# Layer 0 of a four-layer convolution stack: 128 KB transfers in one queue, spread over each slot's products

## The chip, the cores and the metric

The kernel runs on one core of a Trainium2 chip. Its five engines run their own instruction streams: TensorE (PE; its weight loads are shown apart as PEld), VectorE (DVE), ScalarE (ACT), GpSimd (POOL) and SyncE (SP). Transfers between DRAM and the on-chip memory (SBUF) are issued by SP and by ACT and run on 16 DMA engines. The metric is the device time of one execution in microseconds (us). Lower is better.

## The reference, cut to what matters

The input x has 4 images of 16 frames of 512 x 512 float32. Four layers follow, each "x + f(groupnorm(x))". Only layer 0 is touched by the change. It treats the frames as a time series: each output frame is made from a frame and its two neighbours.

```
def _conv_reflect(x, w, bias, dil, pad):
    xp = jnp.pad(x, ((0,0),(0,0),(pad,pad),(pad,pad)), mode='reflect')
    out = conv(xp, w, rhs_dilation=(dil, dil))        # 3 channels in, 1 out, 5 x 5 taps
    return out + bias

def _denoise_block(x, w1, b1, w2, b2, w3, b3, a, b, c):
    trip = _triplets(x)                               # frames t-1, t, t+1
    o = a * _conv_reflect(trip, w1, b1, 1, 2) + b * _conv_reflect(trip, w2, b2, 2, 4) + c * _conv_reflect(trip, w3, b3, 4, 8)
    return jnp.tanh(o)

# layer 0
y = _denoise_block(_gn(x), ...blk1...)
z = _denoise_block(y, ...blk2...)
x = x + z
# layers 1 to 3: x + conv3x3(quantised gn(x)), x + box17x17(gn(x)), x + fft-convolution(gn(x))
```

## The kernel before

Layer 0 goes image by image. For each image the first convolution (`conv` 0, x to y) is done in four groups of four frames, and then the second (`conv` 1, y to z) in four groups: 32 groups in all. A group has six **slots**, p = 0 to 5, so there are 192 slots. In each slot TensorE forms one product (`products`, line 499): 14 steps n of 16 matmuls in 32 x 32 tiles, which the chip runs as 448 matmul instructions. The six products of a group are combined on DVE (a fast algorithm for the three taps in time), so DVE makes six combined frames before (`early`, `late`, `zeroth`, lines 446 to 484) and puts the results together after (`gather`, lines 510 to 552). ACT applies tanh (`activated`). The order of all instructions is written out by hand: each engine runs its stream in exactly the order in which `slot` (line 633) emits it.

PSUM has two product buffers, so product s+2 needs the product of slot s to be gathered. Frames sit in ten SBUF buffers. Tiles of x come from a pool `x` of six buffers of 512 KB (`xr` frames to convolve, `rim` borders, `xs` for the statistics of the next image, `xb` for the final addition). Results y and the reordered z share a pool `rb` of two buffers.

What moves, and on which queue:

- **Loads on SP, through `load` (line 198).** A half of an x frame is one transfer of 512 KB (`load_half`, line 212). A frame of y (`y_frame`, line 390) comes back from DRAM as eight transfers of 132 KB, six edge columns of 16.5 KB and two small ones for the mirrored border. Two shuffles on DVE (lines 409 and 410) then mirror the border columns; they are emitted right behind these loads, in the same slot.
- **Spacing.** `products` keeps the last matmul of each of its 14 steps as a mark. `load` counts the bytes of the slot and makes each transfer wait for one of these marks, one mark further per 190,000 bytes (`PACE`):

```
at = self.marks[min(self.moved // PACE, len(self.marks) - 1)]
self.tc.add_manual_dep(ins, at.name, AFTER, reason="transfers spread over the slot")
```

- **Stores on ACT.** A frame of y leaves in the slot after it is made, in two halves of the partitions, 528 KB each (`y_out`, line 578), at two places of ACT's stream. A frame of the result x1 (`z_out`, line 588) passes three slots: its `xb` halves are loaded where z is transposed, in the next slot `finish` adds on DVE, and one slot later `leave` issues two stores of 512 KB from ACT and sums for the statistics. In an image's last group `leave` comes with `finish`. None of these stores waits for a mark.

`later(n, f, what)` puts a function into slot now + n, where `do(what)` runs it at one of four places of the slot ("stores", "rows", "rest", "last"). `fetch` (line 417) requests frames for the next group: in the second convolution's middle groups frame 2 in p = 0, frame 4 in p = 1, frame 3 in p = 2, frame 5 in p = 4. Results come out in the order i = 2 (p = 4), 1 (p = 5), 0 (p = 0 of the next group), 3 (p = 1).

Of the kernel before, what the change touches and what calls it, by code (L numbers as in the profile page):

```python
# [20 lines left out]
P = 128  # L21
B, C, H, W = 4, 16, 512, 512
# [11 lines left out]
ORDER = (1, 2, 3, 4, 0, 5)  # L34
KN = 9 * 264
NFRAMES = 10
PACE = 190000
AFTER = mybir.DependencyInfo(mybir.DependencyClass.Sync, mybir.DependencyReason.SCHED_ONLY)
HELD = 6

# [81 lines left out]
class Layer0:  # L122
# [12 lines left out]
    def __init__(self, k, ctx, x1):  # L135
        self.k, self.tc, self.nc, self.a, self.x1 = k, k.tc, k.nc, k.a, x1
        tc = self.tc
        self.pools = {}
        for name, bufs in (("frames", 1), ("w", 1), ("sum", 1), ("ra", 2), ("rb", 2), ("x", 6), ("ek", 1)):
            self.pools[name] = ctx.enter_context(tc.tile_pool(name=f"l0{name}", bufs=bufs))  # L140
        self.psum = ctx.enter_context(tc.tile_pool(name="l0ps", bufs=2, space=PSUM))
        self.mv = k.stats.tile([P, NBG, 2], F32, name="mv1")
        self.top = k.stats.tile([P, B, C, 2], F32, name="top1")
        self.low = k.stats.tile([P, B, C, 2], F32, name="low1")
        self.frame_is = k.load(k.stats, "c_frame_is")
        self.parity = k.load(k.stats, "c_parity")
# [4 lines left out]
        self.marks, self.moved = [], 0  # L151


    def weights(self):
# [40 lines left out]
            self.nc.scalar.dma_start(self.w[q][PX * i : PX * i + PX], self.w_dram[conv, :, q])  # L195


    def load(self, to, src):

        ins = self.nc.sync.dma_start(to, src).ins  # L200
        if self.marks:
            at = self.marks[min(self.moved // PACE, len(self.marks) - 1)]
            self.tc.add_manual_dep(ins, at.name, AFTER, reason="transfers spread over the slot")
        self.moved += 4 * int(np.prod(src.shape))

    def load_x(self, b, t, half, name):

# [2 lines left out]
        return xt  # L210

    def load_half(self, xt, b, t, half):
        self.load(xt, self.a["x"][b, t].rearrange("(p T s) w -> T p (s w)", T=2, s=2)[half])

    def finish_stats(self, b, mv, lo=0):

# [62 lines left out]
    def rest_of_first(self, n, p):  # L279

        if n == -1 and p == 0:
            for t in (HELD, HELD + 1):
                self.load_ahead(t)
        for _ in range(1 if n < 0 and p < 4 else 2):
# [46 lines left out]
    def load_rims(self, b, t0):  # L331

        nc = self.nc
        raw = self.pools["x"].tile([P, 2, W], F32, name=f"rim_{b}_{t0}", tag="x")
        x = self.a["x"][b, t0 : t0 + 4]
        for r in range(4):
            for side in range(2):
                at = PX * r + 16 * side
                if (r, side) in ((0, 0), (3, 1)):
                    for s in range(2):  # L340
                        top = 8 - s if side == 0 else H - 2 - s
                        rows = x[:, top : top - 7 if top > 7 else None : -2, :]
                        self.load(raw[at : at + 16, s, :], rows)
                else:
                    r0 = P * r - 8 if side == 0 else P * r + P
                    self.load(
                        raw[at : at + 16].rearrange("p s w -> p (s w)"),
                        x[:, r0 : r0 + 8, :].rearrange("f (m s) w -> f m (s w)", s=2),
                    )
        return raw  # L350
# [39 lines left out]
    def y_frame(self, t):  # L390

        nc = self.nc
        fr = self.free.pop(0)
        v, y = fr.rearrange("p (k r) -> p k r", r=264), self.y[t]
        for c in range(4):
            at = PX * c
            lo, hi = slice(at, at + 16), slice(at + 16, at + PX)
            self.load(v[lo, 1:9], y[hi])
            self.load(v[hi, 0:8], y[lo])
            if c > 0:  # L400
                self.load(v[lo, 0], y[at - 16 : at, 7])
            if c < 3:
                self.load(v[hi, 8], y[at + PX : at + PX + 16, 0])

        self.load(v[0:9:8, 0], y[16:25:8, 0])
        self.load(v[119:P:8, 8], y[103:112:8, 7])
        left = [16 + p + 8 - 2 * (p % 8) if p < 16 and p % 8 else p for p in range(PX)]
        right = [p - 16 + 6 - 2 * (p % 8) if p >= 16 and p % 8 < 7 else p for p in range(PX)]
        nc.vector.stream_shuffle(v[0:PX, 0], v[0:PX, 0], left)
        nc.vector.stream_shuffle(v[96:P, 8], v[96:P, 8], right)  # L410
        return fr


# [72 lines left out]
    def products(self, gr, p):  # L486
# [4 lines left out]
        self.marks, self.moved = [], 0  # L491
# [86 lines left out]
    def y_out(self, gr, i):  # L578
# [1 line left out]
        for to, odd in gr["rim"]:  # L580
            self.stt(to, odd, self.parity[:, 1:2], to)
        gr["rim"].clear()
        y, z = self.y[4 * gr["g"] + i], gr["out"].pop((i, 0))
        for n, what in enumerate(("stores", "rows")):
            at = slice(64 * n, 64 * n + 64)
            self.later(1, partial(nc.scalar.dma_start, y[at], z[at]), what)

    def z_out(self, gr, i):

        nc, b, t = self.nc, gr["b"], 4 * gr["g"] + i  # L590
        zr = self.pools["rb"].tile([P, 2, 2, W], F32, name=f"zr_{b}_{t}", tag="rb")
        xs = []
        for h in range(2):
            z = gr["out"].pop((i, h))
            nc.vector.transpose(zr[:, h].rearrange("p s (k j) -> p k s j", j=16), z.rearrange("p (k r) -> p k r", r=32))
            xs.append(self.load_x(b, t, h, "xb"))

        def finish():
            for h in range(2):
# [10 lines left out]
        def leave():  # L610
# [21 lines left out]

    def slot(self, n, p):

        self.now = 6 * n + p
# [45 lines left out]
    def begin(self, gr):  # L681
# [1 line left out]
        if gr["conv"]:  # L683
            self.out_sums = [self.k.stats.tile([P, 2 * C], F32, name=f"osum{b}_{i}", tag=f"osum{i}") for i in range(2)]
        else:
            self.y = scratch(self.k.dram, f"y_{b}", [C, P, 8, 264])

    def run(self):
        self.groups = [
            {"b": b, "conv": conv, "g": g, "d": {}, "v": {}, "m": {}, "out": {}, "rim": []}  # L690
            for b in range(B)
            for conv in range(2)
            for g in range(4)
# [5 lines left out]
        with self.tc.manual_schedule():  # L699
            self.first()  # L700
            for g in range(-1, n + 1):
                for p in range(6):
                    self.slot(g, p)
                    if g < 1:
                        self.rest_of_first(g, p)
        return self.result()

    def result(self):
# [919 lines left out]
```

## Time and profile before

| what | value |
|---|---|
| median of 3 runs | 5569.73 us (5559.56 to 5571.75) |
| the profiled execution, its own time | 5572.08 us |
| its span | 5570.3 us |
| mean granted TensorE clock | 0.978 |
| first matmul of layer 0 | 80.7 us |
| last matmul of layer 0 | 3177.3 us |
| bytes moved | 860.92 MB, 155 GB/s on average |

One execution is taken apart. PE, PEld, DVE, ACT and POOL have busy times; a row of the groups gives line, engine and operation, the tile written and the tiles read, the number of instructions, busy us and mean ns, and behind the second bar the idle time just before them with what ended it. "Issue" there means idle time in which the engine waited for nothing that the profile shows. q1 is SP's transfer queue, q10 is ACT's, and q8 carries instructions. SPq and ACTq are the issuing of transfers. A row of waits gives the waiting engine and line, what it waited for, total us, number, and the longest.

Two lines of the chain of work that ended last say which engine and which lines carry the end:

```profile
PE 84%; issue 5%; ACT 4%; DVE 4%; DMA 2%; SPq 1%; ACTq 0%; DVEq 0%
PE m L499 50%; PE l1p L915 10%; PE l2p L999 5%; PE u L1464 4%; PE s L1405 4%; PE u L1405 4%; PE u L1427 2%; PE pt L1439 2%; ACT l2n L1017 2%; ACT l2s L1056 2%; PE l2p L1051 1%; SPq L200 1%; DVE frame L415 1%; DMA frame<-y 0%; PE pr L1449 0%
```

### The profile page before, as it was taken

Reading aid. Unit: us, or ns where it says so; the run is one execution under the profiler, and the core shown is the slowest. Engines: PE = TensorE matmul, PEld = TensorE weight load, DVE = VectorE, ACT = ScalarE, POOL = GpSimd, SP = SyncE. Lnnn points to the kernel's source line nnn. Section 1 sums busy time; section 2 is a strip of 40 time slices with the busy share of each in tenths; the row PEclk is TensorE's granted clock in tenths of the full one; section 3 lists DMA queues with packets and bytes.
Section 4 is the critical chain, followed back from the end, with each engine's and each line's share of the span. In section 5 each row is a group of like instructions: output and inputs, shape, how many; then the busy total and the mean of one; then the engine's idle time right before and its main releaser. Section 6 shows DMA issues by size and latency. Waiting matters only on the chain.

```text
span 5570.3 us, 267073 instructions
## 1 busy us (share of the span) xinstructions
PE 5105.7 (92%) x125040; PEld 3556.9 (64%) x125040; DVE 4044.1 (73%) x4738; ACT 2611.6 (47%) x4143; POOL 6.1 (0%) x18
## 2 busy tenths in 40 slices
PE   3999999999999989989999788887999979999999
PEld 2665665666675656666666545554887866777776
DVE  7766889657987659897678854445555568888887
ACT  2533335433345523443122444443665656666665
POOL 0000000000000000000000000000000000000000
PEclk9999999999999999999999999998999999999999
DMA  5555545565445555544454377876565655555554
GB/s 192 136 147 129 153 139 153 142 150 137 122 151 160 142 131 143 150 124 118 89 132 126 117 198 209 214 209 191 199 214 192 214 176 137 143 145 149 148 144 119
DMA packets 373827, 860.92 MB, mean 155 GB/s; under 512 B 52209, under 2 KB 74353, under 8 KB 356081
## 3 DMA queue, kind: packets, MB, share of 16 engines
q1 hardware_dynamic: 317072, 694.76, 44.1%
q10 hardware_dynamic: 55648, 149.08, 9.4%
q8 instruction: 979, 16.04, 1.3%
q14 instruction: 128, 1.04, 0.1%
HBM read 503.74 MB, written 339.90 MB: 151 GB/s over the span
## 4 chain that ended last, share of the span: by engine, by line
PE 84%; issue 5%; ACT 4%; DVE 4%; DMA 2%; SPq 1%; ACTq 0%; DVEq 0%
PE m L499 50%; PE l1p L915 10%; PE l2p L999 5%; PE u L1464 4%; PE s L1405 4%; PE u L1405 4%; PE u L1427 2%; PE pt L1439 2%; ACT l2n L1017 2%; ACT l2s L1056 2%; PE l2p L1051 1%; SPq L200 1%; DVE frame L415 1%; DMA frame<-y 0%; PE pr L1449 0%
## 5 line engine op out<-in xcount | busy, mean ns | idle before, releaser
L499 PE MATMUL m<-frame,l0w 32*32 32x512 f32 x86016 | 2920.8, 608 | 257.1 <-issue 151.7
L499 PEld LDWEIGHTS m<-frame,l0w 32*32 32x32 f32 x86016 | 1968.4, 104 | 1208.6 <-issue 604.0
L415 DVE SCALAR_TENSOR_TENSOR frame<-frame,frame 128x2376 f32<-128x2376 f32 x232 | 606.6, 2625 | 4.7 <-PE m L499 0.4
L915 PE MATMUL l1p<-l1q,l_wt 32*32 32x512 f32 x12288 | 489.2, 603 | 109.6 <-issue 68.1
L915 PEld LDWEIGHTS l1p<-l1q,l_wt 32*32 32x32 f32 x12288 | 274.4, 103 | 266.0 <-issue 186.0
L1039 DVE TENSOR_TENSOR l2o<-l2x,l2p 128x512 f32<-128x512 f32 x256 | 172.6, 674 | 283.1 <-PE l2p L999 283.1
L617 ACT ACTIVATE junk<-xb,neg 128x1024 f32<-128x1024 f32 x256 | 294.1, 1149 | 80.1 <-DVE top L601 38.2
L532 ACT COPY C<-m 128x1024 f32<-128x1024 f32 x64 | 61.6, 1014 | 537.2 <-PE m L499 408.7
L999 PE MATMUL l2p<-k_c_band,l2n 128*128 128x144 f32 (+1 forms) x2048 | 275.1, 295 | 36.5 <-DMA l2x<-x 15.5
L999 PEld LDWEIGHTS l2p<-k_c_band,l2y 128*128 128x128 f32 x2048 | 256.8, 190 | 75.0 <-issue 54.3
L999 PEld LDWEIGHTS l2p<-k_c_band,l2n 128*128 128x128 f32 x2048 | 262.2, 197 | 48.6 <-ACT l2n L1017 41.4
L999 PE MATMUL l2p<-k_c_band,l2y 128*128 128x144 f32 (+1 forms) x2048 | 284.3, 292 | 6.0
L901 DVE TENSOR_SCALAR l1t<-l1t 128x2048 f32<-128x2048 f32 x64 | 78.5, 1226 | 271.2 <-ACT l1t L900 271.2
L900 ACT ACTIVATE l1t<-l1x,l1own,l1own 128x1024 f32<-128x1024 f32 x128 | 151.8, 1233 | 237.4 <-DMA l1x<-x 234.6
L1464 PE MATMUL u<-k_c_hil,zt 128*128 128x128 f32 x2048 | 256.0, 279 | 0.0
L384 DVE STREAM_TRANSPOSE frame<-xp 128x1056 f32<-128x1056 f32 x128 | 161.6, 1278 | 127.0 <-ACT xp L358 127.0
L1464 PEld LDWEIGHTS u<-k_c_hil,zt 128*128 128x128 f32 x2048 | 238.5, 192 | 2.1 <-issue 0.8
L1440 ACT COPY zt<-pt 128x512 f32<-128x512 f32 x256 | 131.5, 601 | 210.3 <-PE pt L1439 210.3
L1028 ACT COPY l2y<-l2p 128x512 f32<-128x512 f32 x256 | 149.7, 585 | 169.1 <-PE l2p L999 169.1
L1370 DVE TENSOR_TENSOR xc<-l3n,k_c_tab 128x2048 f32<-128x2048 f32 x64 | 146.7, 2292 | 109.6 <-ACT l3n L1354 109.6
L915 PE MATMUL l1p<-l1x,l_wt 32*32 32x512 f32 x4088 | 213.3, 632 | 0.0
L1483 DVE SCALAR_TENSOR_TENSOR l3o<-u,l3t 128x256 f32<-128x256 f32 x512 | 192.8, 430 | 23.4 <-ACT l3t L1475 21.0
(302 smaller groups left out, 6553.0 us busy)
## 6 DMA issues: line engine op xcount, KB each, us to landing
y<-y ACTq DMA_DIRECT2D x128, 528.0 KB
frame<-y SPq DMA_DIRECT2D x512, 132.0 KB
xb<-in_x SPq DMA_DIRECT2D x128, 512.0 KB
x<-xb ACTq DMA_DIRECT2D x128, 512.0 KB
x<-l1o SPq DMA_DIRECT2D x256, 256.0 KB
l2x<-x SPq DMA_DIRECT2D x64, 1024.0 KB
x<-l2o SPq DMA_DIRECT2D x64, 1024.0 KB
l3x<-x SPq DMA_DIRECT2D x256, 256.0 KB
```

The source lines that it names most:

```text
L384: nc.vector.transpose(v[:, :, 4 + h : 68 : 2], xp)
L415: self.nc.vector.scalar_tensor_tensor(o, x, f, y, ALU.mult, ALU.add)
L499: ins = nc.tensor.matmul(ps[PX * j : PX * j + PX, i, :].rearrange("p (k r) -> p k r", r=64), w[rows, n], v[rows, k0 : k0 + 8, r0 : r0 + 64 ...
L617: nc.scalar.activation(junk, xs[h], f, bias=neg, accum_out=self.out_sums[n][:, 2 * t + h : 2 * t + h + 1])
L900: nc.scalar.activation(t[:, at], x[:, at], AF.Identity, bias=own[1], scale=own[0])
L915: nc.tensor.matmul(ps[32 * j : 32 * j + 32, b, :], wt[rows, a, d], qs[v % 3][rows, k, d : d + W] if d < 3 else raws[v][rows, k], start=(n ...
L999: nc.tensor.matmul(ps[:, lo:hi], lhs[:, k, at : at + P], band[:, j : j + hi - lo], start=(k == 0), stop=(k == 3), skip_group_check=True,)
L1028: nc.scalar.copy(yts[i][:, wb, :], ps)
L1039: nc.vector.tensor_add(o[:, hb, :], xt[:, hb, :], ps)
L1405: nc.tensor.matmul(ps[b][32 * j : 32 * j + 32], f[rows, n, j, :], x[rows, j, :], start=(i == 0), stop=(i == 2 and tag == "s"), skip_group_ ...
L1464: nc.tensor.matmul(po[:, bass.ts(k, P)], zt[:, b, k ^ 1, :], hil[:, k, :], start=False, stop=(k == 3), skip_group_check=True,)
L1483: nc.vector.scalar_tensor_tensor(o[:, v].rearrange("p k u -> p u k"), po[:, HW:W].rearrange("p (u k) -> p u k", u=2), s, t.rearrange("p (u ...
```

## The change

- All loads of layer 0 are collected per slot, and so are the y stores and most x1 stores. At the end of the slot `transfers` issues them from SP, loads first and then stores. Each waits for the mark that lies as far in the slot as its bytes lie in the slot's sum.
- A half of an x frame moves in four pieces of 32 partitions (128 KB), and so does a half of x1. A frame of y is stored in four pieces of 264 KB, each with two of the eight columns of all partitions.
- y in DRAM gets a pitch of 536 floats for every 528, and its loads are written as rows of 528 floats (2,112 bytes) in place of 2,112 floats (8,448 bytes).
- The two mirror shuffles run one slot after the loads.
- The xb loads come one slot earlier, except in an image's last group and for i = 3. The y store of i = 3 comes three slots after the frame is made, in place of one.
- While an image's last group is under way and in the group behind it (`last_of_image`), x1 stores stay on ACT in 512 KB.

```diff
-    def load(self, to, src):
-
-        ins = self.nc.sync.dma_start(to, src).ins
-        if self.marks:
-            at = self.marks[min(self.moved // PACE, len(self.marks) - 1)]
-            self.tc.add_manual_dep(ins, at.name, AFTER, reason="transfers spread over the slot")
-        self.moved += 4 * int(np.prod(src.shape))
+    def move(self, to, src, what="loads"):
+
+        if self.moves is None:
+            self.nc.sync.dma_start(to, src)
+        else:
+            self.moves[what].append((to, src))
+
+    def transfers(self):
+
+        moves = self.moves["loads"] + self.moves["stores"]
+        sizes = [int(np.prod(src.shape)) for _, src in moves]
+        for n, (to, src) in enumerate(moves):
+            ins = self.nc.sync.dma_start(to, src).ins
+            if self.marks:
+                at = self.marks[len(self.marks) * sum(sizes[:n]) // sum(sizes)]
+                self.tc.add_manual_dep(ins, at.name, AFTER, reason="transfers spread over the slot")
+        self.moves = {"loads": [], "stores": []}
...
     def load_half(self, xt, b, t, half):
-        self.load(xt, self.a["x"][b, t].rearrange("(p T s) w -> T p (s w)", T=2, s=2)[half])
+        src = self.a["x"][b, t].rearrange("(p T s) w -> T p (s w)", T=2, s=2)[half]
+        for r in range(0, P, PX):
+            self.move(xt[r : r + PX], src[r : r + PX])
...
         fr = self.free.pop(0)
-        v, y = fr.rearrange("p (k r) -> p k r", r=264), self.y[t]
+        v, y = fr.rearrange("p (k r) -> p k r", r=264), self.y[t, :, :, 0:528]
+        first, last = y[:, 0, 0:264], y[:, 3, 264:528]
         for c in range(4):
             at = PX * c
             lo, hi = slice(at, at + 16), slice(at + 16, at + PX)
-            self.load(v[lo, 1:9], y[hi])
-            self.load(v[hi, 0:8], y[lo])
+            for to, src in ((v[lo, 1:9], y[hi]), (v[hi, 0:8], y[lo])):
+                self.move(to.rearrange("p (a k) r -> p a (k r)", k=2), src)
...
-        nc.vector.stream_shuffle(v[0:PX, 0], v[0:PX, 0], left)
-        nc.vector.stream_shuffle(v[96:P, 8], v[96:P, 8], right)
+
+        def mirror():
+            nc.vector.stream_shuffle(v[0:PX, 0], v[0:PX, 0], left)
+            nc.vector.stream_shuffle(v[96:P, 8], v[96:P, 8], right)
+
+        self.later(1, mirror)
...
-        y, z = self.y[4 * gr["g"] + i], gr["out"].pop((i, 0))
-        for n, what in enumerate(("stores", "rows")):
-            at = slice(64 * n, 64 * n + 64)
-            self.later(1, partial(nc.scalar.dma_start, y[at], z[at]), what)
+        y = self.y[4 * gr["g"] + i, :, :, 0:528]
+        z = gr["out"].pop((i, 0)).rearrange("p (a k) r -> p a (k r)", k=2)
+        wait = 3 if i == 3 else 1
+        for a in range(4):
+            self.later(wait, partial(self.move, y[:, a], z[:, a], "stores"))
...
             for h in range(2):
-                nc.scalar.dma_start(to[h], xs[h].rearrange("p (s w) -> p s w", s=2))
+                x = xs[h].rearrange("p (s w) -> p s w", s=2)
+                if self.last_of_image:
+                    nc.scalar.dma_start(to[h], x)
+                for r in () if self.last_of_image else range(0, P, PX):
+                    self.move(to[h][r : r + PX], x[r : r + PX], "stores")
...
+        self.last_of_image = (n - 7) % 8 < 2
...
-        self.do("stores")
-
+        for i, at in enumerate((6, 5, 4, 7)):
+            of = cur if p >= 4 or p == 3 and i == 2 else last
+            early = of and of["g"] < 3 and i != 3
+            if of and of["conv"] and p == (at - early) % 6:
+                of["xb"][i] = [self.load_x(of["b"], 4 * of["g"] + i, h, "xb") for h in range(2)]
...
-            self.y = scratch(self.k.dram, f"y_{b}", [C, P, 8, 264])
+            self.y = scratch(self.k.dram, f"y_{b}", [C, P, 4, 536])
...
                     if g < 1:
                         self.rest_of_first(g, p)
+                    self.transfers()
```

More of the change, by code (lines that the diff above doesn't have):

```diff
@@ L36 @@
 NFRAMES = 10
-PACE = 190000
 AFTER = mybir.DependencyInfo(mybir.DependencyClass.Sync, mybir.DependencyReason.SCHED_ONLY)
@@ L150, in __init__ @@
         self.todo, self.gn = {}, {}
-        self.marks, self.moved = [], 0
+        self.marks, self.moves = [], None
     def weights(self):
@@ L281, in rest_of_first @@
         if n == -1 and p == 0:
+            self.transfers()
             for t in (HELD, HELD + 1):
                 self.load_ahead(t)
+            self.transfers()
         for _ in range(1 if n < 0 and p < 4 else 2):
@@ L342, in load_rims @@
                         rows = x[:, top : top - 7 if top > 7 else None : -2, :]
-                        self.load(raw[at : at + 16, s, :], rows)
+                        self.move(raw[at : at + 16, s, :], rows)
                 else:
                     r0 = P * r - 8 if side == 0 else P * r + P
-                    self.load(
+                    self.move(
                         raw[at : at + 16].rearrange("p s w -> p (s w)"),
@@ L397, in y_frame @@
             lo, hi = slice(at, at + 16), slice(at + 16, at + PX)
-            self.load(v[lo, 1:9], y[hi])
-            self.load(v[hi, 0:8], y[lo])
+            for to, src in ((v[lo, 1:9], y[hi]), (v[hi, 0:8], y[lo])):
+                self.move(to.rearrange("p (a k) r -> p a (k r)", k=2), src)
             if c > 0:
-                self.load(v[lo, 0], y[at - 16 : at, 7])
+                self.move(v[lo, 0], last[at - 16 : at])
             if c < 3:
-                self.load(v[hi, 8], y[at + PX : at + PX + 16, 0])
-        self.load(v[0:9:8, 0], y[16:25:8, 0])
-        self.load(v[119:P:8, 8], y[103:112:8, 7])
+                self.move(v[hi, 8], first[at + PX : at + PX + 16])
+        self.move(v[0:9:8, 0], first[16:25:8])
+        self.move(v[119:P:8, 8], last[103:112:8])
         left = [16 + p + 8 - 2 * (p % 8) if p < 16 and p % 8 else p for p in range(PX)]
         right = [p - 16 + 6 - 2 * (p % 8) if p >= 16 and p % 8 < 7 else p for p in range(PX)]
-        nc.vector.stream_shuffle(v[0:PX, 0], v[0:PX, 0], left)
-        nc.vector.stream_shuffle(v[96:P, 8], v[96:P, 8], right)
+        def mirror():
+            nc.vector.stream_shuffle(v[0:PX, 0], v[0:PX, 0], left)
+            nc.vector.stream_shuffle(v[96:P, 8], v[96:P, 8], right)
+        self.later(1, mirror)
         return fr
@@ L490, in products @@
         w = self.w[q].rearrange("p (n o) -> p n o", o=PX)
-        self.marks, self.moved = [], 0
         for n in range(NPB):
@@ L591, in z_out @@
         zr = self.pools["rb"].tile([P, 2, 2, W], F32, name=f"zr_{b}_{t}", tag="rb")
-        xs = []
+        xs = gr["xb"].pop(i)
         for h in range(2):
@@ L595, in z_out @@
             nc.vector.transpose(zr[:, h].rearrange("p s (k j) -> p k s j", j=16), z.rearrange("p (k r) -> p k r", r=32))
-            xs.append(self.load_x(b, t, h, "xb"))
         def finish():
@@ L633, in slot @@
     def slot(self, n, p):
-        self.now = 6 * n + p
+        self.now, self.moves = 6 * n + p, {"loads": [], "stores": []}
+        self.marks = []
         groups = self.groups
@@ L685, in begin @@
         else:
-            self.y = scratch(self.k.dram, f"y_{b}", [C, P, 8, 264])
+            self.y = scratch(self.k.dram, f"y_{b}", [C, P, 4, 536])
     def run(self):
         self.groups = [
-            {"b": b, "conv": conv, "g": g, "d": {}, "v": {}, "m": {}, "out": {}, "rim": []}
+            {"b": b, "conv": conv, "g": g, "d": {}, "v": {}, "m": {}, "out": {}, "rim": [], "xb": {}}
             for b in range(B)
@@ L705, in run @@
                         self.rest_of_first(g, p)
+                    self.transfers()
         return self.result()
```

## The prediction

> **What bounds the kernel now.** I began with the page's busy times and costliest groups.
>
> ```profile
> PE 5105.7 (92%) x125040; PEld 3556.9 (64%) x125040; DVE 4044.1 (73%) x4738; ACT 2611.6 (47%) x4143; POOL 6.1 (0%) x18
> ...
> q1 hardware_dynamic: 317072, 694.76, 44.1%
> q10 hardware_dynamic: 55648, 149.08, 9.4%
> q8 instruction: 979, 16.04, 1.3%
> ...
> L499 PE MATMUL m<-frame,l0w 32*32 32x512 f32 x86016 | 2920.8, 608 | 257.1 <-issue 151.7
> L499 PEld LDWEIGHTS m<-frame,l0w 32*32 32x32 f32 x86016 | 1968.4, 104 | 1208.6 <-issue 604.0
> ```
>
> TensorE sets the end. Layer 0, the only code that changes, is line 499: by the trace its matmuls start from 80.7 to 3177.3 us, 3096.5 us in 192 slots of 448 matmuls, 16.13 us each. Its shortest slots take 14.2 us. At 14.3 us the 192 would take 2746; the other 350 us are what a change of transfers can touch.
>
> "Issue" is idle time with no wait behind it. The q8 row explains it: 979 packets for 16.04 MB are 16.4 KB each, and 250,080 TensorE instructions (matmuls and weight loads) over 979 are 255. So the instruction stream comes by DMA, one packet per 128 matmuls, on the engines that move the data. TensorE's timeline around 1190 us:
>
> ```profile
> 1184.89 4.51 PE L499 MATMUL m<-frame,l0w 32*32 32x512 f32 x128 [0.59 <-issue]
> 1192.48 14.07 PE L499 MATMUL m<-frame,l0w 32*32 32x512 f32 x377 [3.07 <-issue]
> ```
>
> Between two pauses lie exactly 128 matmuls. The DMA view of 1187 to 1192 us (packets, MB, share of 16 engines):
>
> ```profile
> q10 hardware_dynamic: 110, 0.67, 56.3%
> q1 hardware_dynamic: 149, 0.54, 33.3%
> q8 instruction: 1, 0.02, 1.8%
> ```
>
> The engines are 91% full and the one instruction packet arrives late. I counted all 673 such borders: 247 pause for over 0.2 us; beyond the usual 0.05 us, all pauses come to **255 us**. After a pause TensorE resumes about 1.4 us behind the packet's end. A packet takes 1.2 us, a block of 128 matmuls about 3.9: a packet may start some 1.3 us after the block before it began, and the median start is 1.32. The stream lives on the edge, and traffic decides. With the engines up to 5% full in the 3 us after a block began, the next border paused 0.08 us on average; at 30 to 50% 0.22; at 70 to 90% 0.76; above that 1.53.
>
> The other 95 us (350 - 255) are late frames, above all behind VectorE, as a busy-time table by group shows (from:to, length, busy us of PE, PEld, DVE, ACT, POOL; clock; DMA share; GB/s), and the layer's waits (us in total, times, longest):
>
> ```profile
> 559.90:656.00 96.10, 92.66 (x2704) 61.19 (x2702) 86.59 (x81) 32.30 (x44) 0.00 (x0) 0.98 0.51 140
> 851.80:957.10 105.30, 94.71 (x2689) 60.46 (x2692) 95.68 (x87) 65.78 (x118) 0.00 (x0) 0.95 0.52 161
> 1050.80:1141.50 90.70, 88.80 (x2702) 62.10 (x2705) 66.66 (x52) 47.03 (x84) 0.00 (x0) 1.00 0.52 141
> ```
>
> ```profile
> DVE frame L409 <- DMA frame<-y: 250.4, 40, 17.3
> SPq L200 <- PE m L499: 1762.9, 409, 54.2
> SPq L200 <- DMA x<-xb: 206.4, 65, 10.7
> ```
>
> The group at 560 is in the second convolution: DVE works 86.6 of 96.1 us, and its one large wait there is 8.2 us at line 409, for frame loads that the same slot issued. In the first convolution (1051) it has 24 us free; at an image's start (852) it is full. The SPq row shows that the spreading is real: SP waits for matmuls.
>
> **The change, part by part.**
>
> *Pieces and even spacing.* Now a 512 KB load goes out at once, then nothing for 2.7 marks; y stores (528 KB each) and x1 stores leave ACT unspaced. Slots show it: no transfers, 0.14 us of instruction pauses per slot; 1 MB of spaced loads, 0.7 to 1.1; an x frame beside y stores, 2.5; a y frame beside y stores, 2.8; a y frame and an xb pair, nothing from ACT, 0.75 although that is 2.1 MB. The new order puts 1 to 3.3 MB evenly over 14 marks, in pieces of 128 KB (y stores 264). A piece is two 4 KB packets per engine, 0.32 us at the trace's 159 ns; SP needs 0.33 us to issue one, so hardly two ever queue. No row is this case; the ends are 0.14 (empty) and 1.33 (255/192, today). I take 0.55, nearest the ACT-free rows and somewhat under them for the smaller bursts: 192 x 0.55 = 106. In 32 slots around the ends of images the x1 stores stay in 512 KB on ACT (half of them); there I leave 0.5 more: 16 us. Gain 255 - 122 = **133 us**; ends 0 and 228.
>
> *The skill against this.* The Trainium skill, "Runtime: NRT & Kernel Launch", Instruction fetch mechanics, says that code comes in 16 KiB blocks of 256 instructions, which the packets confirm, and that crossing a block is "mostly hidden". By that this part is worth 0; by the 247 counted pauses up to 228. "DMA: Bandwidth & Descriptors", Rules for kernel authors, asks for 1 MiB or more per DMA. Its 2.0 us fixed cost would make the 3,104 SP transfers of the steady part 6,200 us if paid in turn, over twice the layer. The trace issues 132 KB frame loads every 0.40 us, so the fixed part overlaps. The rows decide.
>
> *Mirror one slot later.* The two shuffles of lines 409 and 410 (0.44 and 0.45 us, 64 frames) stay, but DVE no longer stands before this slot's loads. In the second convolution's middle groups the 8 to 9 us per group vanish; then DVE's 86.6 lies just under TensorE's 6 x 14.85 = 89, which is late next. In the second convolution frame 3, loaded in p=2, is mirrored in p=3 ahead of `early`, its first reader; frame 5, loaded in p=4, in p=5. Of the 95 us I give this **40**. The rest stays: the first group of an image has 95.7 us of DVE work plus 8 us of waits for ACT, so 10 to 12 us above the others, three times; and three groups before it where x frames wait for buffers.
>
> *Issues.* Counting the loops, SP issues 3,104 transfers in place of 1,566 (the first 12 loads become 48 besides), and ACT 232 for 424. At the trace's medians (frame load 0.418, x load 0.328, y store 0.453, x1 store 0.367) the fullest common slot (second convolution, p=1: 16 frame parts, 8 xb, 8 x1) costs 12.2 us of SP. The worst (p=0 of the first convolution's last group: 32 frame parts, 4 stores) costs 15.2, slightly over a slot, and the next has 20. A group of 128 needs some 50 us of 89. At nothing, hidden by matmuls. ACT gets back 128 x 0.45 + 64 x 0.37 = 81 us, but has 47% load: nothing.
>
> *Late stores.* In the first convolution a y tile is stored at its next slot's end (i=3 three slots on), so the tanh that reuses its buffer waits up to some 3 us on ACT, four times a group. Queued behind it are ACT's rim copies, next frame normalisations and PSUM copies, then DVE's rim fix (line 415). The cover is DVE's 24 idle us. 5 us for the whole layer; ends 0 and 12 us in 16 groups = 190 if all cover were gone.
>
> *Moved xb loads; padding.* xb comes one slot earlier in three groups of four: only the wait for its buffer matters, a store at the end of the slot before (p=1, about 2 us of SP). The pitch of 536 keeps y rows in 2,112-byte packets. At 2,048 bytes the trace has 84 ns, so four take about 346 ns against 319 for one of 8,448: 9% more engine time on y, within an engine share near 0.5. Nothing; ends -10 and +20.
>
> **Sum.** 133 + 40 - 5 = 168 us off the profiled execution's 5572.1 (span 5570.3 and 1.8 around it): 5404. The runs shown have their median 2.4 lower: **5400**.
>
> **Rivals.**
>
> *Packets still late (5530).* Sorted by load over the surrounding 16 us, borders at 0.4 to 0.6 pause 0.40 us on average, today's mean; the bytes don't shrink. Then only the mirror pays: 5572 - 40 = 5532, less 2. Against it: at equal bytes, slots without ACT stores pause less.
>
> *All hidden (5310).* Pauses fall to the empty slot's 0.14 (27 us; 20 more at image ends) and 55 of the 95 go: 255 - 47 + 55 = 263, so 5309. For it: one piece of 0.32 us is less than the room. Against it: empty engines are not what a packet meets at 50% load.
>
> *SP as the bound, slower (5720).* Everything stands in one order; a store at the head that waits for data, landing or a free buffer holds all loads behind it. Groups 3 to 6 of each image have 117 transfers on average and take 97.4 us now. At 0.41 us each SP needs 48. If the others gain 4.5 us, it turns slower once a transfer costs 0.87 with its waits (102 us a group); at 0.95: 16 x 13.8 - 16 x 4.5 = +148. For it: the rim row's 0.62 us per issue, SP's 206 us of waits for x1 stores, and y pieces whose rows interleave in DRAM, should they be ordered one behind another. Against it: the y-frame row at 0.418.
>
> **Chances.** Forecast (5340 to 5460) 0.54; late packets 0.20; all hidden 0.12; SP slower 0.10; no effect 0.04. The range for 8 in 10 is 5300 to 5535, which takes in the first three but for their tails; faster cases alone hold most of the chance. 0.2% is 11 us, about what a measurement of this kernel tells from no change: faster 0.86, same 0.04, slower 0.10.
>
> **What would show it.** Right: line 499's "issue" idle on PEld well under 604 and on PE under 100; the group like 560 to 656 at 89 to 91 us with DVE near 87 busy; the wait at the shuffles' line (250 us) almost gone; layer 0 ending near 3010. Unspaced bursts gone: instruction packets starting at most 1.3 us into a block. Wrong: SP's queue waiting mainly for y or x1 landings, DVE's wait moved to `frame<-y` one slot later, or ACT's tanh waiting tens of us for `y<-y`. Layers 1 to 3 should keep their lengths.

## The result, and the profile after

The changed kernel takes **5468.17 us** (median of 4 runs, 5465.28 to 5477.66). The kernel before, run beside it, takes 5569.27. The ratio is 0.9825, 95% interval 0.9808 to 0.9842. In the profiled executions it is 5477.66 against 5572.08: 94 us less, where the prediction's sum said 168.

From the page of the changed kernel, the rows that answer to those shown of before:

```profile
PE 5061.6 (92%) x125040; PEld 3689.3 (67%) x125040; DVE 4040.6 (74%) x4738; ACT 2609.9 (48%) x4143; POOL 6.1 (0%) x18
...
q1 hardware_dynamic: 416944, 797.62, 51.1%
q10 hardware_dynamic: 28000, 46.31, 2.6%
q8 instruction: 979, 16.04, 1.3%
...
PE 82%; DVE 6%; ACT 4%; issue 4%; DMA 3%; SPq 1%; ACTq 0%; DVEq 0%; POOL 0%
...
L516 PE MATMUL m<-frame,l0w 32*32 32x512 f32 x86016 | 2878.1, 608 | 217.2 <-DVE frame L470 99.3
L516 PEld LDWEIGHTS m<-frame,l0w 32*32 32x32 f32 x86016 | 2103.3, 103 | 991.1 <-issue 389.4
```

The 103 MB of stores are gone from ACT's queue q10 and are in SP's q1. The "issue" idle of the weight loads fell from 604 to 389 us. The share of DVE in the chain rose from 4 to 6%, and TensorE's greatest wait is now the 99 us at the start.

Layer 0 runs from 99.3 to 3094.7 us: 2995.4 us in place of 3096.5. I counted the 673 borders between instruction packets again. Pauses beyond 0.05 us come to 96 us in place of 255, and 143 of them are over 0.2 us, in place of 247. Packets start 1.2 to 1.3 us into a block on average (1.64 before) and still take 1.2 us. The timeline of TensorE shows 716 matmuls over at least five borders, without a gap that makes a new row:

```profile
1125.41 24.07 PE L516 MATMUL m<-frame,l0w 32*32 32x512 f32 x716
```

So the part of the change that was to pay most paid more than predicted. The rest went the other way. Here is the whole of it, from the two profiled executions, with the groups counted from 0:

| where | before: us, of it pauses | after: us, of it pauses | pauses | all else |
|---|---|---|---|---|
| up to the first matmul | 80.7 | 99.3 | | +18.6 |
| first and last group | 189.5, 12.2 | 182.7, 1.8 | -10.4 | +3.6 |
| 8 groups 1 and 2 of each image | 740.0, 53.6 | 691.1, 9.3 | -44.3 | -4.6 |
| 16 groups 3 to 6 of each image | 1559.2, 148.1 | 1494.1, 76.7 | -71.4 | +6.3 |
| 6 groups around the three changes of image | 607.9, 41.3 | 627.6, 8.2 | -33.1 | **+52.8** |
| layers 1 to 3 | 2393.0 | 2381.1 | | -11.9 |

Layers 1 to 3 are unchanged code; their 12 us are mostly layer 1, 632 us here and 621 to 643 in other profiles of the same code. At a change of image the last group of the one and the first of the next now take longer together than before, although their pauses have nearly gone. The clock records say where that time lies: TensorE's clock is granted either in full or at half, and in these six groups it is at half for 92 us in place of 48 (79 in a second profile of the changed kernel). At full clock a matmul takes 36 ns there in both kernels, waits included; at half clock it takes 80 ns in place of 70.

The table of busy times in stretches, first the kernel before (from:to, length, busy us of PE, PEld, DVE, ACT, POOL; clock; DMA share; GB/s): 10 us of the start, and the two groups around the second change of image.

```profile
10.00:20.00 10.00, 0.00 (x0) 0.00 (x0) 2.59 (x9) 0.00 (x0) 0.00 (x0) 1.00 1.02 409
...
1528.40:1627.00 98.60, 92.05 (x2718) 70.67 (x2697) 82.77 (x73) 44.88 (x78) 0.00 (x0) 0.96 0.51 159
1627.00:1733.00 106.00, 94.72 (x2687) 62.74 (x2700) 95.83 (x87) 66.52 (x118) 0.00 (x0) 0.94 0.54 162
```

Then the changed kernel: the start, the three groups that answer to those of the prediction, and the two around the same change of image:

```profile
10.00:20.00 10.00, 0.00 (x0) 0.00 (x0) 3.98 (x17) 0.00 (x0) 0.00 (x0) 1.00 0.52 131
...
554.80:651.50 96.70, 90.38 (x2704) 65.17 (x2697) 84.46 (x81) 30.55 (x42) 0.00 (x0) 0.96 0.58 140
846.60:952.60 106.00, 94.71 (x2690) 65.56 (x2700) 94.02 (x87) 64.19 (x114) 0.00 (x0) 0.91 0.53 157
1038.80:1126.40 87.60, 87.20 (x2704) 68.30 (x2683) 69.53 (x53) 48.46 (x87) 0.00 (x0) 1.00 0.47 143
1503.10:1607.90 104.80, 93.33 (x2706) 71.45 (x2690) 86.48 (x75) 48.60 (x82) 0.00 (x0) 0.93 0.47 146
1607.90:1711.80 103.90, 94.69 (x2687) 68.48 (x2692) 92.75 (x86) 63.20 (x112) 0.00 (x0) 0.92 0.53 160
```

The group of the first convolution (1039) came down to 87.6 us, and PE is busy all of it. The group of the second convolution (555) did not move (the mean of the four at its place in an image went from 97.5 to 92.2), and the last group of the image (1503) went from 98.6 to 104.8. The first row of each shows the start: with 12 transfers of 512 KB the engines were full and moved 409 GB/s; with 48 pieces of 128 KB they are half idle at 131 GB/s.

That points at who issues. One line's transfers, before (durations are those of issuing on the queue of SP, in ns, min/median/max):

```profile
L200 SPq DMA_DIRECT2D frame<-y x1024: 302/416/2836, 365.9 to 3041.3; - x171
```

and after:

```profile
L209 SPq DMA_DIRECT2D frame<-y x1024: 307/547/2038, 371.8 to 2969.0; - x171
L209 SPq DMA_DIRECT2D xb<-in_x x512: 310/371/2199, 511.6 to 3104.3; - x171
L209 SPq DMA_DIRECT2D y<-y x256: 319/372/1897, 190.2 to 2811.6; - x128
```

The frame load's median rose from 416 to 547; the other medians are near those that I used. The long tail was there before: one frame load in 7.5 took over 1 us, and their mean was 0.59. Over the 3,092 SP transfers of the layer the mean is now 0.54 us. SP issues for 1,662 us of the layer's 2,995, in place of 859. In the full slots that is too much. Eight slots p = 1 of the second convolution have 32 transfers each. Three to six of the 32 take over 1 us, and all together 19 to 22. From one start to the next it is 0.66 to 0.79 us on average, and the last goes out 8.4 to 14.4 us after the slot has ended. In p = 0 of the first convolution's last group (36 transfers) that is 13.4 to 16.9 us. The last marks also lie at the very end of a slot, so that SP has no time in hand there. The waits of the changed kernel from 80 to 3100 us (engine, line, for what; us, times, longest) show where such a load arrives late:

```profile
DVE y L433 <- ACT y L592: 177.6, 50, 23.9
DVE frame L425 <- DMA frame<-y: 142.4, 16, 13.5
ACT y L586 <- DMA y<-y: 103.0, 22, 10.5
```

and those of SP alone:

```profile
SPq L209 <- PE m L516: 996.8, 1017, 30.3
SPq L209 <- DMA x<-xb: 113.6, 44, 10.4
```

The wait at the shuffles' line fell from 250 us in 40 to 142 in 16. It is not gone: once in each group that feeds the second convolution, frame 3, loaded in p = 2, isn't there when p = 3 mirrors it. SP still waits for matmuls, but for 997 us in place of 1763.

### The profile page after: what moved, and what is told of

The parts are those of the page before. It is cut to its first block, busy times and chain, and to the rows that moved or that the text cites. A ratio compares the mean times of both kernels' runs of the same rounds, so it can differ in the third digit from the quotient of the medians.

```text
span 5475.9 us, 270435 instructions
## 1 busy us (share of the span) xinstructions
PE 5061.6 (92%) x125040; PEld 3689.3 (67%) x125040; DVE 4040.6 (74%) x4738; ACT 2609.9 (48%) x4143; POOL 6.1 (0%) x18
## 3 DMA queue, kind: packets, MB, share of 16 engines
q1 hardware_dynamic: 416944, 797.62, 51.1%
## 4 chain that ended last, share of the span: by engine, by line
PE 82%; DVE 6%; ACT 4%; issue 4%; DMA 3%; SPq 1%; ACTq 0%; DVEq 0%; POOL 0%
PE m L516 48%; PE l1p L944 10%; PE l2p L1028 5%; PE u L1493 4%; PE s L1434 4%; PE u L1434 4%; PE u L1456 2%; PE pt L1468 2%; ACT l2n L1046 2%; ACT l2s L1085 2%; PE l2p L1080 1%; DVE frame L433 1%; DVE l2o L1068 1%; DMA x<-l2o 0%; DVE st L1069 0%
## 5 line engine op out<-in xcount | busy, mean ns | idle before, releaser
L516 PE MATMUL m<-frame,l0w 32*32 32x512 f32 x86016 | 2878.1, 608 | 217.2 <-DVE frame L470 99.3
L516 PEld LDWEIGHTS m<-frame,l0w 32*32 32x32 f32 x86016 | 2103.3, 103 | 991.1 <-issue 389.4
```

The source lines that it names most:

```text
L516: ins = nc.tensor.matmul(ps[PX * j : PX * j + PX, i, :].rearrange("p (k r) -> p k r", r=64), w[rows, n], v[rows, k0 : k0 + 8, r0 : r0 + 64 ...
```

## The experiments

My theory after the result: small pieces free the instruction packets, but VectorE or late x frames at an image's end set the pace there, and SP, busy twice as long, makes the loads trail. The rivals are named in each expectation. The runs went to chips on which the kernel before takes 5526 to 5534 us, so I compare ratios, and the changed kernel has two: 0.9825 and, as a control, 0.9857. The control missed its own expectation (0.981 to 0.984). The table has the numbers that the verdicts rest on, the last four from each run's profile. The intervals of e1, e3, e8, e11 and e12 each overlap with that of one of the two measurements of the changed kernel and miss the other's; those of e4, e6, e7 and e10 lie below both.

| run | ratio to before | 95% interval | first matmul, us | pauses, us | 6 groups at image ends, us | 16 groups 3 to 6, us |
|---|---|---|---|---|---|---|
| kernel before | 1 | | 80.7 | 255 | 607.9 | 1559.2 |
| changed | 0.9825 | 0.9808 to 0.9842 | 99.3 | 96 | 627.6 | 1494.1 |
| changed, again (e5) | 0.9857 | 0.9824 to 0.9891 | 98.8 | 80 | 622.6 | 1471.9 |
| no minima (e1) | 0.9791 | 0.9765 to 0.9817 | 98.9 | 95 | 599.0 | 1479.8 |
| before, no minima (e2) | 0.9895 | 0.9870 to 0.9921 | 80.6 | 222 | 584.4 | 1521.9 |
| x in 256 KB (e3) | 0.9906 | 0.9882 to 0.9931 | 92.4 | 171 | 614.5 | 1502.2 |
| stores on GpSimd (e4) | 0.9760 | 0.9731 to 0.9789 | 97.9 | 87 | 617.3 | 1440.4 |
| the same, no minima (e6) | 0.9735 | 0.9701 to 0.9769 | 99.7 | 94 | 600.3 | 1445.1 |
| e4, first loads whole (e7) | 0.9749 | 0.9721 to 0.9778 | 85.5 | 93 | 614.4 | 1447.1 |
| no marks (e8) | 0.9889 | 0.9856 to 0.9921 | 100.4 | 101 | 650.5 | 1473.5 |
| x whole at ends (e9) | 0.9817 | 0.9791 to 0.9843 | 81.8 | 99 | 613.2 | 1480.0 |
| e9, stores on GpSimd (e10) | 0.9737 | 0.9715 to 0.9758 | 81.3 | 112 | 604.7 | 1442.9 |
| mirror as before (e11) | 0.9873 | 0.9849 to 0.9898 | 99.6 | 64 | 619.1 | 1487.7 |
| y not padded (e12) | 0.9795 | 0.9769 to 0.9822 | 97.9 | 90 | 620.3 | 1456.9 |

### Is VectorE the bound around image ends? (e1, e2, e6)

The statistics of an image need minima of each finished half; without them VectorE has some 38 us less to do in four groups around an image's end. e1 takes them from the changed kernel, e2 from the kernel before, e6 from e4 (below).

```diff
+        self.nc.vector.memset(self.low, -3.0)
-                nc.vector.tensor_reduce(self.low[:, b, t, h : h + 1], xs[h], AX.X, ALU.min)
```

> The changed kernel without the minimum over each finished half frame (128 VectorE reductions of 1.22 us; the tile of minima is filled with a constant instead, so the bound that layer 1 quantises with rests on the maximum alone). Theory 1: from the second group of an image's second convolution to the first group of the next image (groups 5 to 8) VectorE is the bound: 352 us of work and 38 us of its waits fill the 395 us before and after the change. Taking 39 us of work out of each stretch then shortens it until TensorE is the bound at 4 x (85.8 + 2.5) = 353: some -38 us three times and -5 in each of the last image's three, in all -100 to -130: 5340 to 5370. Theory 2: the rest is instruction packets and contention of transfers, VectorE is covered: no change, 5458 to 5478.

> The kernel before without the same reductions (minima left out in the same way). Theory 1: the stretch of groups 5 to 8 is bound by VectorE here too, but with its pauses for instruction packets TensorE needs 4 x (85.8 + 7.7) = 374 of the 396, so some -20 us three times and little else: -50 to -80, 5490 to 5520; and the distance to the changed kernel without them grows from 101 us to about the 159 us by which the pauses shrank, less the start. Theory 2: no change, 5560 to 5575, and the distance stays near 101.

> Stores on GpSimd and no minimum (as before: minima left out, a constant in their place). Theory 1, as the first four runs left it: the stretch of groups 5 to 8 is bound by VectorE's work plus its waits for frames that SP brings late; without the minimum alone the waits grew from 14 to 28 us and ate most of the 38 us; without late frames alone it fell by 11. With both it must fall by far more than the sum of the two (24 us): to 4 x 88.5 = 354 plus some 8 us of waits for x frames, so 358 to 366 in place of 395 to 397, and layer 0 to some 2835 us. Rival: both are independent small gains that add up: 370 us, layer 0 some 2885.

e1 won 0.3 to 0.7% over the changed kernel, 19 to 37 us, where VectorE as the sole bound would give 100 to 130. Its two groups around the change of image:

```profile
1472.10:1572.30 100.20, 90.97 (x2705) 68.08 (x2688) 78.16 (x68) 47.69 (x81) 0.00 (x0) 0.96 0.51 153
1572.30:1671.50 99.20, 91.52 (x2690) 67.75 (x2699) 83.47 (x78) 63.48 (x113) 0.00 (x0) 0.94 0.56 168
```

DVE lost 8 and 9 us of work there, and the groups 4.6 and 4.7: the rest became idle time, 22 us of 100 in the first. e2 won over 1% on the kernel before, with the six groups down 23.5 us. Theory 1 had the distance between e2 and e1 grow beyond 101 us; it fell to 61. With the stores moved off SP as well (e6), the four groups around an image's end stayed at 375 to 385 us, where the theory had 358 to 366, and the layer took 2919 us, where the theory had 2835 and its rival 2885. So VectorE's work has a part in the pace at image ends, but it is not the bound by itself. That part of my theory fell.

### Piece size or marks? (e3, e8)

e3 moves x in 256 KB, e8 keeps the pieces and drops every wait for a mark.

```diff
-        for r in range(0, P, PX):
-            self.move(xt[r : r + PX], src[r : r + PX])
+        for r in range(0, P, 64):
+            self.move(xt[r : r + 64], src[r : r + 64])
```

```diff
-            if self.marks:
+            if False:
```

> The changed kernel with x halves (loads and x1 stores) in two pieces of 256 KB in place of four of 128; y transfers as they are. Theory 1: SP pays per transfer (0.65 us from one to the next in loaded slots), so fewer transfers end its lateness: the second convolution's p=1 slots fall from 32 to 24, the start's loads take half as long (-10 us), waits at the shuffles' line fall from 142 to under 110 us: -10 to -30, 5440 to 5460, with pauses up by some 10 to 20 us from today's 96. Theory 2: pieces of 128 KB are what keeps packets early; pauses rise by 40 or more and the time by 20 to 40: 5490 to 5510.

> The changed kernel without the waits for marks: the same pieces in the same order on SP, each issued as soon as its buffer and data allow. If the even spacing keeps instruction packets early, pauses rise from 96 us to 130 to 180 and the time by 10 to 60 us. If the size of the pieces does it (SP's own pace spaces them), pauses stay under 120 us; frames come earlier, the waits at the shuffles' line fall under 60 us and the stretch of groups 5 to 8 gains 10 us each: -20 to -40.

Doubling the piece brings the pauses from 80 or 96 to 171 us and loses 0.5 to 0.8%. Dropping the marks brings them only to 101. So it is the size of a piece that lets the packets through, and not the even spacing; SP's own pace between the pieces, which stays in both runs, may have a part. Without the marks the frame loads also come in time, as expected, although SP issues for longer still (1,856 us). The wait at the shuffles' line in e8:

```profile
DVE frame L425 <- DMA frame<-y: 3.7, 2, 3.0
```

So SP makes these loads late only together with marks that hold it to the slot. The expected 20 to 40 us did not follow: e8 loses 0.3 to 0.6%, most of it around image ends (650.5 us). The waits of SP in e8 show what took the place of the marks:

```profile
SPq L209 <- ACT xp L371: 282.9, 27, 19.7
SPq L209 <- DMA x<-xb: 242.1, 43, 26.9
SPq L209 <- DVE y L433: 211.0, 11, 50.8
```

SP now runs to the head of its list early and stands there for a buffer that ACT, a store or DVE has yet to free. Why that costs 28 us at image ends I did not settle.

### Is SP the bottleneck? (e4, e7, e10, e12)

e4 issues the stores from GpSimd and leaves the loads on SP, with the same marks. e7 and e10 add larger first loads (e10 also around image ends). e12 takes the padding of y away.

```diff
-            ins = self.nc.sync.dma_start(to, src).ins
+            queue = self.nc.sync if n < len(self.moves["loads"]) else self.nc.gpsimd
+            ins = queue.dma_start(to, src).ins
```

```diff
-            self.y = scratch(self.k.dram, f"y_{b}", [C, P, 4, 536])
+            self.y = scratch(self.k.dram, f"y_{b}", [C, P, 4, 528])
```

> The changed kernel with the y and x1 stores issued from GpSimd, each at the same mark, and the loads alone on SP. Theory 1: loads stand no longer behind the stores of the slot before, SP has 87 us less to issue per image's four heavy groups, the waits at the shuffles' line fall from 142 us to under 80, the stretches of groups 5 to 8 gain 5 to 10 us each: -20 to -45, 5425 to 5450. Theory 2: three queues share the 16 engines again and instruction packets come later: pauses rise from 96 us, +10 to +40. Theory 3 (late stores hold ACT's tanh and so VectorE): stores at the same marks land at the same time, no change.

> The changed kernel as it is, beside the next three on one chip, so that they can be set against it and not only against the kernel before. Every theory: 0.981 to 0.984 of the kernel before.

> Stores on GpSimd, and the 12 half frames that are loaded at the start whole (512 KB), as before the change. Theory: 48 pieces in place of 12 transfers cost the start 18.6 us, as SP waits as long per transfer and each carries a quarter; the first matmul goes back from 98 to 80 to 83 us, everything after it as with stores on GpSimd alone: 15 to 19 us less than that, 0.972 to 0.974 of the kernel before. Rival: the late start is due to the order of the queue behind those loads (rims, xs in pieces), then at most 5 us.

> The changed kernel with y rows in DRAM 528 floats apart instead of 536, so that four rows lie behind one another and could again be moved as 8,448 bytes. My prediction priced the padding at nothing (ends -10 and +20 us). If packets become 8,448 bytes and the queue's row shows fewer of them, with the engines' share up to 9 per cent lower on y: the time within 10 us of the changed kernel, ratio 0.984 to 0.988. If the packet size decides how late instruction packets come: pauses in layer 0 up by over 20 us and the ratio 0.989 or more.

e4 is 0.7 to 1.0% faster than the changed kernel. Its transfers, two of its waits, and the group of the second convolution:

```profile
L210 POOL DMA_DIRECT2D y<-y x256: 539/539/1592, 187.5 to 2747.9; - x128
L210 POOL DMA_DIRECT2D x<-xb x256: 533/533/560, 558.1 to 2915.2; - x128
```

```profile
DVE frame L426 <- DMA frame<-y: 102.1, 15, 13.5
ACT y L587 <- DMA y<-y: 66.5, 18, 12.3
```

```profile
549.00:636.30 87.30, 87.30 (x2705) 68.86 (x2690) 86.09 (x81) 32.18 (x45) 17.07 (x32) 1.00 0.59 155
```

512 stores left SP, which now issues for 1,385 us in place of 1,662. The same group that took 96.7 us takes 87.3, with PE busy all of it and DVE 86.1: this is the group that the prediction described. Over the 16 groups 3 to 6 the time without pauses is 1374.5 us, against 1411.2 before the change and 1417.3 after it (1409 in the control); TensorE is never at half clock there, in place of 48 us before and 27 after. The gain was there, and the stores on SP hid it. By which way is open: e4 takes their issuing time from SP, lets the loads out from behind them, and lets the stores themselves land sooner. The wait for frames fell from 142 us (127 in the control) to 102, not under 80 as expected, and tanh's wait for y stores from 103 to 67. The Trainium skill, "DMA: Bandwidth & Descriptors", Issuing engines are not separate DMA queues, says that several issuing engines save only the issuing time, "usually small relative to the DMA itself". Here a piece of 128 KB takes 0.37 us to issue, and with 1,662 us on one queue that was not small.

e12 goes the same way without moving a transfer. Its frame loads:

```profile
L209 SPq DMA_DIRECT2D frame<-y x1024: 302/411/2156, 366.8 to 2914.6; - x171
```

Its queue q1 has 392,368 packets in place of 416,944: four rows that lie behind one another go as one packet again. The median issue of a frame load falls from 547 to 411 ns, the mean from 0.66 to 0.53, which takes 130 us off SP; the wait at the shuffles falls from 127 us in the control to 103. It is 0.3 to 0.6% faster than the changed kernel, and so outside both of its expectations; against the first of the two measurements the intervals overlap, against the control they just miss each other. The pauses hardly differ (90 against 80 and 96), so the size of y's packets does not decide them. The engines' time is not lower either: 51.8% of 5419.0 us against 51.2% of 5441.4. That leaves issuing as what the padding costs.

e7 brings the first matmul back from 97.9 to 85.5 us (expected: 80 to 83), but in time it can't be told from e4.

### Image ends and the start (e9, e10)

e9 moves x halves whole at the start and in the two groups around an image's end.

```diff
-        for r in range(0, P, PX):
-            self.move(xt[r : r + PX], src[r : r + PX])
+        step = P if self.last_of_image else PX
+        for r in range(0, P, step):
+            self.move(xt[r : r + step], src[r : r + step])
```

> The changed kernel, with x halves as one transfer of 512 KB again at the start and in the two groups around each image's end; y frames, stores and all other groups stay as changed. Theory A (around image ends the many small transfers make the x frames late, and that is what lengthened the two groups from 202.6 to about 208 us): the two groups fall to 202 or below, three times, and the start gives back 12 to 18 us: 30 to 48 us less than the changed kernel (ratio to before 0.977 to 0.980). Theory B (a chain of VectorE and ACT work sets the pace there whatever the transfers): the two groups stay within 2 us of 207.5 and only the start gains: 12 to 18 us less (ratio 0.982 to 0.984). Theory C (512 KB transfers make instruction packets late again there): the pauses in these groups grow by over 8 us for each image end and the groups by some of that; ratio 0.985 or more.

> Both: x halves whole at the start and around image ends, and the stores issued from GpSimd instead of SP. If the two gains lie in different stages they add: the stores' 57 us (5459.4 to 5402.9) and whatever the whole halves give beyond that. Theory A: ratio 0.968 to 0.972, the two groups around an image's end at 200 or below. Theory B: 0.973 to 0.975, like the run with the stores on GpSimd and only the first loads whole (0.9749).

The start came back fully (81.8 us). The six groups fell to 613.2 us, 9 under the control, by a trade: the pauses in them rose from 7 to 27 us, and everything else fell from 616 to 587. So both Theory A and Theory C have a part. The many pieces make more than half of the 53 us that image ends lost, but larger ones bring the late packets back. In time e9 is 0.1 to 0.4% under the changed kernel, within the intervals. e10 (0.9737) landed where Theory B put it, on e7, though the pieces do cost something at its ends too (604.7 us against 617.3 in e4). Of the kernels that compute everything it has the lowest ratio, about 1% under the changed one; its interval overlaps with those of e4 and e7. Its two groups at the second change of image take 201.2 us together, against 204.6 before the change and 208.7 after it:

```profile
1447.50:1546.80 99.30, 88.64 (x2707) 69.66 (x2691) 84.56 (x74) 46.65 (x80) 0.00 (x0) 0.98 0.47 153
1546.80:1648.70 101.90, 93.21 (x2690) 66.48 (x2692) 92.24 (x86) 62.60 (x112) 1.68 (x3) 0.94 0.49 163
```

Stores on GpSimd, whole halves at the ends and y without padding were not tried together.

### What is the moved mirror worth? (e11)

The shuffles are put back behind the transfers of their own slot.

```diff
-        self.later(1, mirror)
+        self.mirrors.append(mirror)
```

> The changed kernel with the two mirror shuffles put back into the slot of the loads they mirror, behind the slot's transfers. My prediction priced the move at 40 us; the waits at the shuffles' line fell from 250 to 142 us. If the move is worth its price: 30 to 60 us slower than the changed kernel (ratio 0.992 to 0.997), because loads that are now spread to the slot's end and beyond leave VectorE standing until then, in all slots that load y frames. If VectorE has enough slack to take the wait in the loads' slot: within 10 us of the changed kernel (0.984 to 0.988). Since the loads now trail the slot, it may be worse than in the kernel before: over 100 us slower (above 1.004).

The wait at their line rose to 211 us in 40, and yet the time is within 0.2% of the control (0.5% above the first measurement). In groups 3 to 6 the time without pauses rose by 18 to 27 us, and TensorE was at half clock for 58 us in place of 14 and 27, while the pauses fell by 11 to 25. By these profiles moving the mirror paid about 20 us, half of its price in the prediction, and most of it came back as later packets; in the timed runs it paid nothing that can be told from the control.

## Why the prediction was right in direction and short in size

The measured 5468 lies outside the forecast's own case (5340 to 5460) and inside the range for 8 in 10. It would lie further off if two errors had not met: the pauses gave 26 us more than the sum had, and the terms below lost 100.

**Instruction packets (-133): right, and more.** The pauses fell by 159 us. The value taken, 0.55 us per slot, was 0.50. It was chosen between 0.14 and 1.33, and that it came so near is in part luck, for its reason was half wrong: the size of the pieces does it (e3), the spacing adds next to nothing (e8). The Trainium skill's "mostly hidden" ("Runtime: NRT & Kernel Launch", Instruction fetch mechanics) holds for most borders and not for the sum: of 673 borders 426 before and 530 after pass without a pause over 0.2 us, but 255 and 96 us were in the open.

**But 33 of these 159 us shortened nothing.** They lay in the six groups at image ends, which took longer without them. e3 and e9 have 20 to 25 us more pauses there than the control, and are 8 and 9 us shorter. I had seen that those groups are 10 to 12 us above the others for another reason, and still took their pauses off the end.

**Issues, "at nothing, hidden by matmuls": the step that failed.** I priced each transfer at its median and only asked if the sum fits into the slot. The 12.2 us of the fullest common slot became 19 to 22. The trace of before held the tail that the median leaves out, and there one frame load started 0.52 us after another at the median, and not the 0.40 that I wrote. And a load must not only be issued within the group, it must land before its reader, while the marks hold a slot's last transfers to its end. The rival with SP as the bound named this mechanism with a break-even of 0.87 us per transfer; at 0.66 to 0.79 in the full slots the kernel stays faster, but it pays. e4 and e12 take issuing time from SP in two unlike ways, and groups 3 to 6 come down to 1440 and 1457 us, from 1494 and 1472 in the two profiles of the changed kernel. Those two differ by more than e12 gains on the second, so e12 rests on its timed runs.

**Mirror (-40): did not come.** Groups 3 to 6 took 6 us more outside the pauses (2 less in the control). With the stores off SP (e4) they take 37 less than before. That is near 40, but no run has the mirror as before on that stream, so how much of it is the mirror's is not shown.

**Startup, 12 loads into 48: mentioned and not priced; +18.6 us.** My own 0.33 us for each of 36 further issues would have said 12. e9 takes 17 of it back.

**Image ends: "the rest stays" was wrong; +53 us outside the pauses.** e9 and e10 show that the pieces are over half of it. What I left out altogether is the clock: a wait of TensorE counts again when half clock follows it. At half clock for 92 us in place of 48, TensorE can have lost up to 22 us more in these groups than before (half of the difference); in e9, with 61 us, up to 7 of the 20 by which its 587 exceed 567. That is a sum and not an experiment, since waits and half clock come together there. The rest stays open. e4 and e10 are 5 and 8 us lower than the control and e9, but two profiles of the changed kernel differ by 5.

**Late stores (+5): not held, and open in size.** ACT's tanh waits 103 us for y stores in place of 13. 59 of these lie in the four last groups of the first convolution, which take 385 us together; with the stores on GpSimd (e4) that wait is 23 us and the groups take 366 (382 in the control). So late stores may have a part in what e4 won. In the groups 1 and 2 of an image, where I looked for cover, tanh waits too, and they run at 86 to 88 us: there the cover held.

**Padding ("nothing", -10 to +20): a small miss.** It costs 17 to 34 us, the lower end not clear of noise, and by e12 through the issuing and not through the engines, where I looked. There I set four packets of 86 ns against one of 8,448 bytes in 319 ns; that was a fast one, and their median on q1 is 555.

**Moved xb loads:** nothing in the runs speaks for a cost or a gain.

Of the signs I named, "issue" on PEld well under 604 and on PE under 100 were seen (389 and 91). Packets at most 1.3 us into a block came in part: the mean is there, but 255 of 672 start later (345 before). Not seen were the group at 89 to 91 us (96.7, and 87.3 only in e4), the shuffles' wait almost gone (142) and the layer's end near 3010 (3095). Of the signs against it, DVE's wait moved one slot later and the tanh waiting for stores were seen, and they belong to the loss.

## What to carry to other kernels

Where code streams in by DMA beside data, cut the transfers until an instruction packet fits between them, and count the idle time that is left at the block borders. Then price the issuing queue by the mean and not by the median, slot by slot, until the last load has landed where it is read; a queue that is 55% busy on average can trail by most of a slot. A pause that lies in the shadow of another wait is no gain when it goes.

## What the runs showed of the hardware

- Issuing one transfer from SP takes 0.31 to 0.62 us at the median, by kind, and over 1 us for one in eleven of the layer (three to six of 32 in the full slots). The 16 transfers of a frame take 547 ns at the median when the rows of the large ones are packets of 2,112 bytes, and 411 when they are joined into 8,448 (e12; 416 before).
- From GpSimd a store takes 539 or 533 ns at the median, with hardly a tail for x1 (560 at most).
- At the start SP's 48 pieces of 128 KB kept the engines at 52% and 131 GB/s from 10 to 20 us, where 12 of 512 KB gave 102% and 409 GB/s.
- Two profiles of the same changed kernel differ by 30 us in layer 0 (2995.4 and 2965.3), 16 of them in pauses: differences of single profiles below that say little without the timed runs.
- After a stretch without a matmul start TensorE's clock can fall to half for 3.4 us or a multiple of it, as at 1193.2 us before, behind the pause that the prediction shows. In layer 0 of the 14 profiles, 2 of 411 stretches of 1 to 2 us were followed by half clock within 4 us, and 93 of 193 of 2 to 5 us.
